# Two octets of a graph layer summed from SBUF instead of gathered: a change to a relational graph kernel

## The chip, the cores and the metric

The kernel runs on one core of one Trainium2 chip. The metric is device time in microseconds (us) from launch to end, the median of several executions. A profiled execution gives each engine's instructions with start and duration. The engines: TensorE (PE; its weight loads are PEld), VectorE (DVE), ScalarE (ACT), GpSimd (POOL) and SyncE (SP). "L766" is line 766 of the kernel's file.

## The reference

Two layers of a relational graph convolution with eight relations, 12500 nodes of 128 features and 200000 edges sorted by destination, then a residual and a layer norm:

```python
def _rgcn_conv(x, src, dst, et, basis, comp, root, bias):
    W = jnp.einsum('rb,bio->rio', comp, basis)
    xw = jnp.einsum('ni,rio->nro', x, W)
    msgs = xw[src, et]
    seg = dst * N_REL + et
    summed = segment_sum(msgs, seg, N_NODES * N_REL)
    cnt = segment_sum(ones, seg, N_NODES * N_REL)
    mean = summed / maximum(cnt, 1.0)[:, None]
    agg = mean.reshape(N_NODES, N_REL, HIDDEN).sum(axis=1)
    return agg + x @ root + bias
h = x
for l in range(2):
    h = relu(_rgcn_conv(h, ...)) + h
out = layernorm(x + h)
```

So each node takes, over its incoming edges, the source's row times the matrix of the edge's relation, divided by how many of its edges have that relation.

## The kernel before

The 200000 edges are cut into 1563 tiles of 128 edges, one edge per partition, and eight tiles make an octet (`Q = G = 8`, `NQ = 196` octets). The nodes are cut into 98 blocks of 128 (`NT`).

**Gathers.** For each tile GpSimd issues one indirect DMA that fetches 128 rows of 512 bytes, one per edge, into a slot of `rows` (L766, in `gather`, L738). A ring of seven buffers of one octet each holds them; in the main loop the gathers of octet q+5 are issued at octet q (`gathers`, L786), and an instruction of GpSimd waits until the buffer that it fills has been used. A few tiles are "lone": their rows are fetched one by one by SP and ACT (`lone_rows`, L679; 56 tiles of layer 1, 64 of layer 2). The last six octets are gathered under a tighter rule (`LATE`, `CLOSE`).

**Layer 1** gathers rows of x. For each tile VectorE makes a one-hot `dm` (L1188) from the numbers 0 to 127 (`cols`, which stand in PSUM), the edge's place `kr` (16 destinations x 8 relations) and its weight `w` (one over the count). TensorE multiplies rows and one-hot (`means`, L1288), which gives the means per destination and relation, turned; the relations' matrices follow (`product`, L1320), then a second one-hot `pl` puts the 128 results of an octet where their destinations belong (`place`, L1351). The result h is kept turned, features by nodes, in `hT`, a part of `arena` in SBUF. From h a table `y_d` in HBM is made with one row for each node and relation, h times the relation's matrix (`table`, L1408).

**Layer 2** gathers rows of `y_d` (index `idy`), so that a row is already a message. The loop at L1813 runs over the octets q: gathers of octet q+5, lone rows, `add_rows(q)` (L1447), `onehot(1, q + 2)` (L1844), then one step of the layer norm from `todo`. `add_rows` is eight matmuls on TensorE, row buffer times one-hot of 256 columns (`near`, L1463), summed in a PSUM accumulator `acc[k]`; a block of 128 nodes takes two octets, and opens with the node's own row times `root` (L1466). Three accumulators are used in turn (`acc_b`, L1443). When a block is complete, `finish` (L1359) adds the carry and the bias on VectorE and, one octet later, the ReLU and the residual (L1395). For every eight blocks `norm` (L1534) appends steps of the layer norm; one of them (L1571) is on ACT, and VectorE's L1575 waits for it.

**Order.** `Plan` (L300) writes out one order of instructions per engine, by hand: each engine takes its own in turn, and waits on semaphores for what others write or read. The one-hots have two buffers in layer 2, so `onehot(1, q + 2)` waits until the sums of octet q are done. From its column 128 x HA on, `arena` holds the edges' raw numbers in layer 1 (`early`, L524); `hT` takes 98 x 128 columns.

Of the kernel before, what the change touches and what calls it, by code (L numbers as in the profile page):

```python
# [299 lines left out]
class Plan:  # L300
# [90 lines left out]
    last = None  # L391
# [37 lines left out]
def ordered_path(  # L429
# [26 lines left out]
    P = 128  # L456
# [41 lines left out]
    def keep(shape, dtype, name):  # L498
        return const.tile(shape, dtype, name=name)
# [50 lines left out]
    def h_cells(j):  # L550

        return [("h", j)] + [c for a, b, cells in over.values() if a < (j + 1) * P and b > j * P for c in cells]

    comp_sb = keep([P, L * R * NB], F32, "comp_sb")
    first = keep([P, B], F32, "first")
# [50 lines left out]
    def vec(emit, reads=(), writes=()):  # L606
        plan.add("DVE", emit, reads, writes)
# [4 lines left out]
    def pe(emit, reads=(), writes=()):  # L612
        plan.add("PE", emit, reads, writes)
# [124 lines left out]
    def gather(l, q):  # L738
        if q >= NQ:
            return  # L740
# [419 lines left out]
    def rows_of(j):  # L1160
        return min(P, N - j * P)
# [11 lines left out]
    def onehot(l, q, g=None):  # L1173

        if q >= NQ and (g is None or g < 0):
            return
# [231 lines left out]
    def table(j):  # L1408
# [5 lines left out]
        def half(k):  # L1414
# [8 lines left out]
            def second_step(copy=copy):  # L1423
# [69 lines left out]
    def first_sums():  # L1493
# [4 lines left out]
        k = NT - 1  # L1498
        a, ac = acc[k] = acc_b[k % 3]
        m = rows_of(k)  # L1500
# [312 lines left out]
    for q in range(NQ):  # L1813
# [11 lines left out]
        if opens:  # L1825
            acc[k] = acc_b[k % 3]
        if q == NQ - 1:
# [105 lines left out]
```

## Time and profile before

| | |
|---|---|
| median of 3 executions | 3782.29 us (3776.45 to 3784.11) |
| the profiled execution's own time | 3776.47 us |
| its span, first to last instruction | 3774.6 us |
| granted TensorE clock, mean | 0.821 |
| POOL | busy 2840.8 us, 75% |
| TensorE matmuls | busy 2394.9 us, 63% |
| VectorE | busy 1692.9 us, 45% |
| ScalarE | busy 354.4 us, 9% |
| mean HBM traffic | 75 GB/s over the span |

Layer 2's gathers begin near 1890 us. A group's row reads: line, engine, operation, written tile `<-` read tiles, shapes, count `|` busy us, mean ns of one `|` idle time of the engine before them, and what ended it. In a timeline a row is start us, duration us, engine, line and operation. "Issue" is time in which an engine waited for nothing that the profile shows.

### The profile page before, as it was taken

To read this page: it belongs to the slowest core of one execution; us is meant where nothing else is said; L and a number is where in the kernel's file an instruction comes from. 1 tells how busy PE (TensorE), PEld (TensorE's weight loads), DVE (VectorE), ACT (ScalarE), POOL (GpSimd) and SP (SyncE) were. 2 spreads that over 40 slices of the span, in tenths; PEclk is the share of its full clock that TensorE was granted. 3 is DMA by queue.
4 is the path that set the end of the run, shared out by engine and by line. 5 is a ranking of instruction groups with operands and counts; after the bars stand their busy time and mean duration, and the time that the engine had idled before them with its cause. 6 is when DMAs were issued, how large, how long until landed. Compare 5 with 4: busy or idle time off the path is not lost.

```text
span 3774.6 us, 63987 instructions
## 1 busy us (share of the span) xinstructions
PE 2394.9 (63%) x11367; PEld 1919.0 (51%) x11367; DVE 1692.9 (45%) x4754; ACT 354.4 (9%) x795; POOL 2840.8 (75%) x3015
## 2 busy tenths in 40 slices
PE   5777657777767767776755654655555556565556
PEld 3566645555555556665544443444444445444344
DVE  5656424544434333343343443543544444444445
ACT  1111212211111111111100000000000000000000
POOL 7777777777777777777777777777777777777776
PEclk7999879999888888789887777877877777777777
DMA  4222233433323233323332222223223232232222
GB/s 125 56 62 62 56 89 102 126 106 106 100 79 89 84 89 89 84 83 96 93 86 55 56 61 62 61 62 67 61 62 67 56 67 62 61 68 61 62 61 69
DMA packets 157204, 286.78 MB, mean 76 GB/s; under 512 B 67548, under 2 KB 90846, under 8 KB 156790
## 3 DMA queue, kind: packets, MB, share of 16 engines
q0 software_dynamic: 96224, 197.26, 22.6%
q10 hardware_dynamic: 31051, 55.68, 4.5%
q1 hardware_dynamic: 29515, 29.70, 3.0%
q14 instruction: 322, 2.64, 0.2%
q8 instruction: 92, 1.51, 0.2%
HBM read 223.72 MB, written 58.65 MB: 75 GB/s over the span
## 4 chain that ended last, share of the span: by engine, by line
POOL 41%; issue 17%; DMA 14%; PE 9%; ACTq 8%; SPq 4%; ACT 3%; DVE 2%; POOLq 0%; DVEq 0%
POOL rows L766 41%; DMA rows<-y_d,idy 12%; ACTq L702 6%; SPq L702 4%; ACTq L697 2%; PE s L1288 2%; ACT sT L623 2%; PE y L1320 1%; PE pt L1418 1%; ACT y_row L623 1%; SPq L697 1%; PE s L1463 1%; DVE dm L1188 1%; PE ct L959 1%; PE ct L960 1%
## 5 line engine op out<-in xcount | busy, mean ns | idle before, releaser
L766 POOL DMA_INDIRECT rows<-in_x_dram,idx x1507 | 1423.9, 945 | 462.2 <-issue 455.8
L766 POOL DMA_INDIRECT rows<-y_d,idy x1499 | 1414.8, 944 | 457.6 <-issue 443.3
L1188 DVE TENSOR_SCALAR dm<-cols,near,w 128x256 f32<-128x256 f16 x1563 | 723.5, 534 | 749.2 <-PE s L1463 424.4
L1463 PE MATMUL s<-dm,rows 128*128 128x256 f32 x1984 | 627.9, 478 | 444.7 <-DMA rows<-y_d,idy 328.2
L1463 PEld LDWEIGHTS s<-dm,rows 128*128 128x128 f32 x1984 | 472.5, 247 | 569.9 <-issue 305.8
L1188 DVE TENSOR_SCALAR dm<-cols,kr,w 128x128 f32<-128x128 f16 x1563 | 525.3, 401 | 206.8 <-PE s L1288 177.3
L1288 PEld LDWEIGHTS s<-dm,rows 128*128 128x128 f32 x3014 | 435.9, 225 | 273.6 <-DMA rows<-in_x_dram,idx 222.7
L1288 PE MATMUL s<-dm,rows 128*128 128x128 f32 x3014 | 458.7, 312 | 171.9 <-DMA rows<-in_x_dram,idx 168.3
L1463 PE MATMUL ct<-dm,rows 128*128 128x256 f32 x1008 | 357.4, 521 | 305.0 <-DMA rows<-y_d,idy 190.1
L1463 PEld LDWEIGHTS ct<-dm,rows 128*128 128x128 f32 x1008 | 265.7, 274 | 379.2 <-issue 202.8
L1320 PE MATMUL y<-w_sb,sT 128*128 128x128 f32 x1968 | 264.9, 292 | 52.4 <-ACT sT L623 52.4
L1320 PEld LDWEIGHTS y<-w_sb,sT 128*128 128x128 f32 x1968 | 251.3, 207 | 61.4 <-ACT sT L623 60.3
L1418 PE MATMUL pt<-w_sb,arena 128*128 128x512 f32 (+1 forms) x386 | 227.1, 673 | 64.7 <-DVE y_row L626 43.9
L1351 PE MATMUL po<-pl,ys 128*128 128x256 f32 x392 | 140.1, 442 | 156.0 <-ACT sT L623 150.9
L623 ACT ACTIVATE sT<-s 128x512 f32<-128x512 f32 x391 | 213.4, 606 | 83.3 <-PE s L1288 83.0
L626 DVE COPY y_row<-pt 128x512 f32<-128x512 f32 x56 | 38.7, 691 | 365.5 <-PE pt L1418 365.5
L623 ACT ACTIVATE y_row<-pt 128x512 f32<-128x512 f32 (+1 forms) x139 | 83.0, 597 | 1043.3 <-PE s L1288 560.3
L1320 PE MATMUL ct<-w_sb,sT 128*128 128x128 f32 (+1 forms) x1168 | 162.3, 299 | 0.7 <-ACT sT L623 0.7
L1351 PEld LDWEIGHTS po<-pl,ys 128*128 128x128 f32 x392 | 65.3, 202 | 184.3 <-ACT sT L623 174.1
L1320 PEld LDWEIGHTS ct<-w_sb,sT 128*128 128x128 f32 (+1 forms) x1168 | 157.5, 216 | 1.3 <-ACT sT L623 1.1
L1571 ACT ACTIVATE st<-st,eps 128x8 f32<-128x8 f32 x12 | 3.7, 309 | 1560.3 <-DMA sT<-y_d 1507.0
L1372 DVE TENSOR_TENSOR po<-po,carry 128x128 f32<-128x128 f32 x98 | 29.0, 296 | 251.5 <-PE s L1288 230.4
(214 smaller groups left out, 1290.7 us busy)
## 6 DMA issues: line engine op xcount, KB each, us to landing
sT<-y_d SPq DMA_DIRECT2D x4096, 0.5 KB
sT<-y_d ACTq DMA_DIRECT2D x4096, 0.5 KB
y_d<-y_row ACTq DMA_DIRECT2D x96, 512.0 KB
mixer<-in_x_dram ACTq DMA_DIRECT2D x2304, 0.5 KB
rows<-in_x_dram,idx POOLq DMA_INDIRECT x1507
rows<-y_d,idy POOLq DMA_INDIRECT x1499
jmp<-in_x_dram SPq DMA_DIRECT2D x1408, 0.5 KB
comp_sb<-in_x_dram SPq DMA_DIRECT2D x1408, 0.5 KB
```

Of the source, the lines that this page charges most:

```text
L623: act(lambda: nc.scalar.activation(out_t, in_t, AF.Copy), reads, writes)
L626: vec(lambda: nc.vector.tensor_copy(out_t, in_t), reads, writes)
L697: _, at = nc.values_load_multi_w_load_instructions(offs[r:r + 1, l * P + j * ch:l * P + (j + 1) * ch], engines=[mybir.EngineType.SP if e = ...
L702: return [eng.dma_start(o[j * ch + i:j * ch + i + 1, :].bitcast(byte), table_b[bass.ds(v, 4 * D)].rearrange("(p d) -> p d", p=1)) for i, v ...
L766: ins.append(nc.gpsimd.indirect_dma_start(out=t[:, i - q * Q, :], out_offset=None, in_=table_t, in_offset=bass.IndirectOffsetOnAxis(ap=ids ...
L959: nc.tensor.matmul(ct[:, :nb, :], id_h, eq[:, s - s0, :nb, main], start=(s == 1), stop=False)
L1188: emits.append(lambda i=i: nc.vector.tensor_scalar(t[:, i - q * Q, :wide], cols[:, :wide], ids[:, i:i + 1], w[:, i:i + 1], op0=ALU.is_equa ...
L1288: last = nc.tensor.matmul(s_b[i // 4][0][:, i % 4, :], lones[i][0] if i in lones else t[:, i, :], d[:, i, :], start=True, stop=True)
L1320: last = nc.tensor.matmul(y[:m], t[:, r, :nt, :].rearrange("p t k -> p (t k)"), w_sb[:, 0, r, :], start=(r == 0), stop=(r == R - 1))
L1351: ins = nc.tensor.matmul(a, o[:m], t[:m], start=opens, stop=last and not root_in)
L1418: pe(lambda: nc.tensor.matmul(hb[:n].rearrange("p r d -> p (r d)"), hT[:, j * P:j * P + n], w_sb[:, 1, k * H:(k + 1) * H, :].rearrange("p ...
L1463: ins = nc.tensor.matmul(a, lones[i][0] if i in lones else t[:, i, :], d[:, i, :], start=(opens and i == 0), stop=(last and i == n - 1 and ...
```

## The change

Octets 96 and 188 of layer 2 (`SUMMED`, 16 tiles, none of them lone) are neither gathered nor given one-hots by `onehot`. Instead their rows are summed up from h in SBUF over many earlier octets: octet 96 during octets 3 to 86, octet 188 during 94 to 178. A load on SP brings the octet's 1024 source numbers to all partitions; VectorE casts them to float32 (`edge`). For each block j of 128 nodes TensorE turns `hT`'s block (`turn`), VectorE copies it out and makes a one-hot of 128 x 1024, block's node against edge's source (`ready`), and TensorE multiplies the two in two matmuls of 512 columns that accumulate over all 98 blocks (`sums`). At the end these sums, rows of h by edge, turned, go through the steps of layer 1 for that octet in the steps `done + 1` to `done + 7`, and `place_sums` adds the octet's result where `add_rows` would have summed the gathered rows. Buffers for it lie in `arena` behind `hT`. A PSUM bank each is taken by the turned blocks and by the two halves of the sums; for that layer 2's accumulators go from three to two, and `y` grows to a whole bank.

```diff
+    SUMMED = {96: (3, 86), 188: (94, 178)}
...
+    edge = later_on(Q * P)
+    hot_b = [(later_on(Q * P), ("hot", i)) for i in range(4)]
+    hn_b = [(later_on(P), ("hn", i)) for i in range(4)]
...
-    y_b = [(psum.tile([P, D], F32, name="y"), ("py", 0))]
+    y_full = (psum.tile([P, 4, P], F32, name="y"), ("py", 0))
+    y_b = [(y_full[0][:, 0, :], y_full[1])]
...
     def gather(l, q):
-        if q >= NQ:
+        if q >= NQ or l == 1 and q in SUMMED:
             return
...
     def onehot(l, q, g=None):
 
-        if q >= NQ and (g is None or g < 0):
+        if q >= NQ and (g is None or g < 0) or l == 1 and q in SUMMED:
             return
...
-             (s_b[1][0].rearrange("p t d -> p (t d)")[:, :2 * P], s_b[1][1]),
-             (ct_b[0].rearrange("p t d -> p (t d)")[:, :2 * P], ct_b[1])]
+             (s_b[1][0].rearrange("p t d -> p (t d)")[:, :2 * P], s_b[1][1])]
+
+    def summed(served, first, end):
+
+        n = end - first + 1
+        takes = {q: [] for q in range(first, end + 3)}
+        for j in range(NT):
+            takes[first + j * n // NT].append(j)
+        halves = (pt_b, y_full)
...
+        done = end + 2
...
+        def turn(q):
+            for j in takes.get(q, ()):
+                m = rows_of(j)
+                b, bc = ct_b
+                pe(lambda j=j, m=m, b=b: nc.tensor.transpose(b[:m, j % 4, :], hT[:, j * P:j * P + m], ident),
+                   [("h", j), "ident"], [bc])
+            plan.mark("PE")
+
+        def ready(q):
+            for j in takes.get(q - 1, ()):
+                m = rows_of(j)
+                (o, oc), (e, ec) = hn_b[j % 4], hot_b[j % 4]
+                vec(lambda j=j, m=m, o=o: nc.vector.tensor_copy(o[:m], ct_b[0][:m, j % 4, :]), [ct_b[1]], [oc])
+                vec(lambda j=j, e=e: nc.vector.tensor_scalar(e, edge, float(-j * P), part_f, op0=ALU.add,
+                                                             op1=ALU.is_equal), ["edge", "part_f"], [ec])
+            plan.mark("DVE")
+
+        def sums(q):
+            for j in takes.get(q - 2, ()):
+                m = rows_of(j)
+                (o, oc), (e, ec) = hn_b[j % 4], hot_b[j % 4]
+                for h, (b, bc) in enumerate(halves):
+                    pe(lambda j=j, m=m, o=o, e=e, h=h, b=b: nc.tensor.matmul(
+                        b.rearrange("p t c -> p (t c)"), o[:m], e[:m, 4 * h * P:4 * h * P + 4 * P],
+                        start=j == 0, stop=j == NT - 1), [oc, ec], [bc])
+
+        def before(q):
+            if q == first - 3:
+                load(g_t.bitcast(I32), bass.AP(tensor=src.tensor, offset=src.offset + served * Q * P,
+                                               ap=[[0, P], [1, Q * P]]), [], [g_c] + fresh)
+            if q == first + 1:
+                vec(lambda: nc.vector.tensor_copy(edge, g_t.bitcast(I32)), [g_c], ["edge"] + fresh)
+            ready(q)
+            if q == done + 1:
+                each_half(lambda h, b, bc: vec(lambda: nc.vector.tensor_copy(g3[:, 4 * h:4 * h + 4, :], b), [bc],
+                                               [g_c]))
+                vec(in_turn([lambda i=i, t=t: nc.vector.tensor_scalar(
+                    d3[:, i, :], cols[:, :P], kr[:, t:t + 1], w[:, t:t + 1], op0=ALU.is_equal, op1=ALU.mult)
+                    for i, t in enumerate(tiles)]), ["cols", ("kr", b0), ("wt", b0)], [d_c])
...
+        def after(q):
+            sums(q)
+            turn(q)
+            if q == done + 2:
+                each_half(lambda h, b, bc: pe(in_turn([lambda i=i: nc.tensor.transpose(
+                    b[:, i, :], g3[:, 4 * h + i, :], ident) for i in range(4)]), [g_c, "ident"], [bc]))
+            if q == done + 4:
+                each_half(lambda h, b, bc: pe(in_turn([lambda i=i: nc.tensor.matmul(
+                    b[:, i, :], r3[:, 4 * h + i, :], d3[:, 4 * h + i, :], start=True, stop=True)
+                    for i in range(4)]), [r_c, d_c], [bc]))
+            if q == done + 6:
+                pe(in_turn([lambda r=r: nc.tensor.matmul(
+                    y_full[0][:, 0, :], s4[:, r].rearrange("p t k -> p (t k)"), w_sb[:, 1, r, :],
+                    start=r == 0, stop=r == R - 1) for r in range(R)]),
+                   [s_c] + [("w", 1, r) for r in range(R)], [y_full[1]])
+            plan.mark("PE")
...
+    def place_sums(q, k, opens, last):
+        t, c = pl.pop(q)
+        o, oc = ys.pop(q)
+        a, ac = acc[k]
...
+            ins = nc.tensor.matmul(a, o, t, start=opens, stop=last and not root_in)
...
     def add_rows(q, k, opens, last, between_last=None):
+        if q in SUMMED:
+            place_sums(q, k, opens, last)
+            return
...
         if opens:
-            acc[k] = acc_b[k % 3]
+            acc[k] = acc_b[k % 2]
...
+        summing(q, 0)
         add_rows(q, k, opens, last)
         onehot(1, q + 2)
+        summing(q, 1)
```

`summing(q, 0)` calls `before(q)` and `summing(q, 1)` calls `after(q)` of the octet being summed.

More of the change, by code (lines that the diff above doesn't have):

```diff
@@ L552, in h_cells, with later_on @@
         return [("h", j)] + [c for a, b, cells in over.values() if a < (j + 1) * P and b > j * P for c in cells]
+    room = [NT * P]
+    room_c = [c for a, b, cells in over.values() if b > NT * P for c in cells]
+    def later_on(n):
+        room[0] += n
+        assert room[0] <= at
+        return arena[:, room[0] - n:room[0]]
+    edge = later_on(Q * P)
+    hot_b = [(later_on(Q * P), ("hot", i)) for i in range(4)]
+    hn_b = [(later_on(P), ("hn", i)) for i in range(4)]
     comp_sb = keep([P, L * R * NB], F32, "comp_sb")
@@ new lines, in ordered_path, with summing, emit @@
+    sums_of = [(s - 1, *summed(s, *SUMMED[s])) for s in sorted(SUMMED)]
+    def summing(q, part):
+        for end, *f in sums_of:
+            if SUMMED[end + 1][0] - 3 <= q <= end:
+                f[part](q)
+    def place_sums(q, k, opens, last):
+        t, c = pl.pop(q)
+        o, oc = ys.pop(q)
+        a, ac = acc[k]
+        root_in = opens and k >= 0
+        reads = [c, oc] + ([("h", k), ("w", 1, R)] if root_in else [])
+        def emit():
+            ins = nc.tensor.matmul(a, o, t, start=opens, stop=last and not root_in)
+            if root_in:
+                ins = nc.tensor.matmul(a[:, :rows_of(k)], w_sb[:, 1, R, :], hT[:, k * P:k * P + rows_of(k)],
+                                       start=False, stop=last)
+            return ins
+        pe(emit, reads, [ac])
+        plan.mark("PE")
@@ L1498, in first_sums @@
         k = NT - 1
-        a, ac = acc[k] = acc_b[k % 3]
+        a, ac = acc[k] = acc_b[k % 2]
         m = rows_of(k)
```

27 lines of the change are left out of this document (added).

## The prediction

> **What bounds the kernel now.** I read the page's busy shares and costliest groups first, then the stretches of layer 2, then the list of waits of GpSimd's engine.
>
> ```profile
> span 3774.6 us, 63987 instructions
> PE 2394.9 (63%) x11367; PEld 1919.0 (51%) x11367; DVE 1692.9 (45%) x4754; ACT 354.4 (9%) x795; POOL 2840.8 (75%) x3015
> L766 POOL DMA_INDIRECT rows<-in_x_dram,idx x1507 | 1423.9, 945 | 462.2 <-issue 455.8
> L766 POOL DMA_INDIRECT rows<-y_d,idy x1499 | 1414.8, 944 | 457.6 <-issue 443.3
> ```
>
> No engine is busy for more than 75%, yet POOL has no free time. Its 3006 gathers take 0.94 us each, and behind each lies a gap put down to "issue", so to nothing that another engine does. The second row gives (1414.8 + 457.6) / 1499 = 1.249 us from one gather to the next. The stretches (one of layer 1, then layer 2) and the waits say the same:
>
> ```profile
> core 0: us, PE busy (x) PEld busy (x) DVE busy (x) ACT busy (x) POOL busy (x), PEclk, DMA share, GB/s
> 400.00:800.00 400.00, 281.66 (x1633) 224.42 (x1634) 166.57 (x505) 72.07 (x160) 302.21 (x321) 0.88 0.34 96
> ...
> 2000.00:3600.00 1600.00, 892.85 (x2911) 703.05 (x2909) 732.70 (x1856) 4.37 (x11) 1208.87 (x1282) 0.76 0.29 62
> engine line waited for: us in total, times, longest us
> POOL rows L766 <- issue: 401.5, 1315, 0.3
> POOL rows L766 <- DMA rows<-y_d,idy: 12.2, 40, 0.3
> POOL rows L766 <- PE s L1463: 1.5, 5, 0.3
> ```
>
> 1600 us of layer 2 hold 1282 gathers, 1.248 us apiece, and no wait of POOL is longer than 0.3 us, which is the ordinary gap under another name. So layer 2 is one unbroken row of gathers: a gather left out is worth 1.249 us, and anything that lengthens a gather is paid in full. TensorE (56% here) and VectorE (46%) have room.
>
> **What the change removes.** 16 gathers that nothing delayed: 16 x 1.249 = 20.0 us, the whole gain. The 16 one-hots and 16 matmul pairs that go with them lie on engines with room and count nothing.
>
> **What it adds on VectorE, and what that does to POOL.** For each of 98 blocks of h, twice over, VectorE copies a turned block out of PSUM, and compares 1024 float32 source numbers in SBUF with the block's 128 rows into another SBUF tile: 196 compares, and two casts of the same width that fill `edge`, 198 wide operations. None of the trace is as wide. Its operations from SBUF to SBUF, with one turned out of PSUM for comparison:
>
> ```profile
> L1046 DVE TENSOR_SCALAR arena<-arena 128x128 f32<-128x128 f32 x13 | 2.9, 222 | 0.2
> L921 DVE CAST arena<-arena 128x512 f32<-128x512 int32 x3 | 1.2, 416 | 0.0
> L1578 DVE TENSOR_SCALAR x_g<-x_g,st 128x128 f32<-128x128 f32 x96 | 25.9, 357 | 0.4
> L626 DVE COPY y_row<-pt 128x512 f32<-128x512 f32 x56 | 38.7, 691 | 365.5 <-PE pt L1418 365.5
> ```
>
> From 128 to 512 columns it is (416 - 222) / 384 = 0.51 ns an element, half of what the copy out of PSUM needs (691 against 416 at the same width). That makes 222 + 896 x 0.51 = 0.68 us for 1024. The new compare has one operand that is a column (`part_f`); L1578 has two and takes 0.13 us more than L1046, so I add half, 0.06: 0.74 us. Bounds: 0.68 without it, 0.80 with both.
>
> The busy time is small (1.2 compares per octet). But these fast operations do something to POOL. Here are six places of the timeline (the profile merges neighbours of a kind); POOL's undisturbed row is 0.94 or 0.95:
>
> ```profile
> 288.60 0.61 DVE L938 TENSOR_SCALAR arena<-arena 128x896 int32<-128x896 int32 x1
> 288.77 1.26 POOL L766 DMA_INDIRECT rows<-in_x_dram,idx  x1 [0.30 <-issue]
> ...
> 698.91 0.22 DVE L1048 TENSOR_SCALAR arena<-arena 128x128 f32<-128x128 f32 x1
> 698.96 0.99 POOL L766 DMA_INDIRECT rows<-in_x_dram,idx  x1 [0.30 <-issue]
> ...
> 147.39 1.10 POOL L766 DMA_INDIRECT rows<-in_x_dram,idx  x1 [0.30 <-issue]
> 147.96 0.41 DVE L921 CAST arena<-arena 128x512 f32<-128x512 int32 x1
> ...
> 155.04 0.95 POOL L766 DMA_INDIRECT rows<-in_x_dram,idx  x1 [0.31 <-issue]
> 155.16 0.62 DVE L938 TENSOR_SCALAR arena<-arena 128x896 int32<-128x896 int32 x1
> ...
> 637.76 0.95 POOL L766 DMA_INDIRECT rows<-in_x_dram,idx  x1 [0.30 <-issue]
> 638.39 0.36 DVE L1048 TENSOR_SCALAR arena<-arena 128x128 f32<-128x128 f32 x1
> ...
> 2511.26 2.14 DVE L1578 TENSOR_SCALAR x_g<-x_g,st 128x128 f32<-128x128 f32 x8
> 2511.88 1.05 POOL L766 DMA_INDIRECT rows<-y_d,idy  x1 [0.30 <-issue]
> ```
>
> At 288.77 a gather starts while a fast operation runs, and is 0.32 us too long. The operation ends at 289.21; 289.21 - 0.32 is 0.12 us into the gather. At 698.96 the operation ends at 699.13, the gather loses 0.05: again 0.12. So about 0.12 us after its start a gather needs something that the operation holds, and waits for its end. At 147.39 the operation starts 0.57 into the gather and ends 0.98 into it, and the gather loses 0.16: a second need, at 0.98 - 0.16 = 0.82 at the latest. At 155.04 the operation runs from 0.12 to 0.74 of the gather, between the two, and nothing is lost; it started no later than the first need and did not stop it, so it holds nothing in its first part. At 638.39 it is the other way round: an operation that starts at 0.63 takes 0.36 and not 0.22, to 0.99, and the gather loses nothing. There POOL holds, from about 0.65 to 0.90 (0.14 late on a flow that would have begun near 0.78). The last pair shows it in layer 2: 1.05 for 0.94.
>
> So a 0.74 us compare holds for its last 0.56 us, say (0.51 ns x 1024 = 0.52 of flow, and its end). Its hold may begin anywhere in a gather's 1.249 us: VectorE's work hangs on landings and matmuls of varying length, and the rows above show it at every phase. In the three parts of a period:
> - beginning at A from 0.12 to 0.65, it ends at A + 0.56 and costs what lies beyond 0.82: 0 to 0.39 us, over the last 0.39 of that stretch, area 0.076;
> - from 0.65 to 0.90 it waits, then ends at 1.46, and the next gather wanted it at 1.37: 0.09 over 0.25, area 0.022;
> - from 0.90 to 1.37 it runs across the next gather's first need: 0.09 to 0.56, mean 0.325 over 0.47, area 0.153.
>
> The sum, 0.251, over 1.249 is 0.20 us per operation, and 198 x 0.20 = 39.8 us. Bounds: with the first need alone, that one row (147.39) being all that shows a loss at the second, 0.175 / 1.249 x 198 = 28 us; with 0.80 us long operations, a hold of 0.62, the same areas are 0.101, 0.038 and 0.181, so 51 us.
>
> The Trainium skill, SBUF — State Buffer, section Who interferes with whom, has a rule for this: a VectorE operation in a two-port mode and a GpSimd instruction take one shared port pair in turn, each for its whole instruction. The trace agrees that they exclude each other, but not on the whole instruction: the 0.62 us operation at 155.16 lies inside a gather and neither is longer for it. What the literal rule would make of the time is the second rival below.
>
> **TensorE.** Each block adds a turn and two matmuls of 512 columns.
>
> ```profile
> L1255 PE MATMUL pt<-ident,x_g 128*128 128x128 f32 x97 | 18.2, 317 | 14.8 <-DVE wide L626 12.8 <-ACT wide L623 1.2 <-DVE idx L898 0.8
> L1418 PE MATMUL pt<-w_sb,arena 128*128 128x512 f32 x384 | 226.0, 673 | 64.7 <-DVE y_row L626 43.9 <-DMA w_sb<-w_d 19.4 <-ACT y_row L623 1.4
> PE ct L1463 <- DVE dm L1188: 67.7, 10, 22.1
> 2514.52 16.10 DMA rows<-y_d,idy
> ```
>
> A float32 matmul is two instructions, so the turn is 2 x 18.2 / 97 = 0.38 us, a wide matmul 2 x 226.0 / 384 = 1.18, and a block 2.7 us. 98 blocks over 84 octets make 3.2 us per octet. An octet lasts 8 x 1499 / 1563 x 1.249 = 9.6 us, of which 56% or 5.3 are taken: 8.5 of 9.6. It fits. What covers it is the ring of seven row buffers: the gathers of octet n need the sums of octet n-7, whose rows land 16.1 us after they are issued (last row) and are then added in some 4 us, so POOL has 7 x 9.6 - 9.6 - 16 - 4 = 37 us of lead, against the longest stall of TensorE, 22 us.
>
> The accumulators go from three to two. A block's sums may now open only when VectorE has taken the block before last (the operation after `finish`), which stands one octet earlier in VectorE's queue than `onehot` two octets ahead. Behind it wait that octet's sums, and behind those POOL's buffers. In the stalls it makes TensorE stop an octet (4 us) earlier: 37 - 22 - 4 = 11 us are left. I take nothing; without the cover the price is the fourth rival's.
>
> `ready` stands in VectorE's queue before the one-hots two octets ahead and waits for the turn behind the previous sums; those one-hots wait for the next sums anyway, which lie later. The load of 512 KB on SP comes four octets, 38 us, before it is read. The closing steps of an octet (8 turns, 16 narrow and 2 x 8 instructions, copies from PSUM) take odd and even octets in turn, with no fast operation in them. The last octets, which set the tail, are unchanged.
>
> **The sum.** -20.0 + 39.8 = +19.8 us. The profiled execution took 3776.5 us (span 3774.6 and 1.9 around it): 3796.3. The median shown, 3782.3, lies 5.8 above that execution; I forecast 3799, in between. Slower, by about 0.5%.
>
> **Rivals.**
> 1. *No holding (faster).* The compare might run at the rate of operations that touch PSUM: then it holds nothing and POOL keeps its 1.249. The time is 3776.5 - 20.0 = 3756.5. For it: no operation with this pair of operands (a constant, then a column) is in the trace. Against: L1578, float32 with columns, does hold. It decides at a mean loss of 20.0 / 198 = 0.10 us per wide operation; above that the change loses.
> 2. *A gather keeps the place for its whole 0.94 us.* A compare that comes in those 76% waits for the gather's end, starts 0.30 us ahead of the next and keeps that one from 1.249 + 0.12 to 0.94 + 0.74: 0.31 us. One that comes in the gap costs 0.31 to 0.61, mean 0.46. Mean 0.35, times 198 is 68.7 us: 3825. Against it is the row at 155.16; for it that a stalled 638.39 ended just past its gather.
> These are the Trainium skill's words in that section, taken literally.
> 3. *Phase.* The compares fall into step with the gathers and mostly pass between the two needs, or mostly do not. Near nothing or 0.56 us each: 3757 to 3887; as both move with every octet's landing I expect the mean.
> 4. *TensorE becomes the bound after VectorE's stalls.* At 8.5 of 9.6 us an octet it gains 1.1 us an octet, 17 in the 16 octets between stalls of 22. What it can't make up, 5 us, would hold up POOL ten times: 50 us more, 3846. Against: TensorE was granted 0.76 of its clock here at 56%, but 0.88 in the quoted stretch of layer 1, where it was busy for 70%; a TensorE that catches up should be faster than 8.5.
>
> **How the numbers follow.** The forecast's own mechanism, with its bounds of 28 to 51 us and either base, 3784 to 3813: 0.66. Rival 1 with the good half of 3: 0.12. Rival 2: 0.10. Rival 4 and the bad half of 3: 0.08. The rest, 0.04, is a loss about equal to the gain. The range 3778 to 3826 takes in the first and the second of these with the last, and leaves the others, 0.20, outside. About 0.2%, 7.6 us, is what a measurement can tell from no change: faster 0.11, nearly all of the 0.12; the same 0.10, which is the 0.04, 0.05 from the lowest end of the forecast's mechanism, and 0.01 of the 0.12; slower 0.79, the rest.
>
> **What would show it.** POOL's gathers of layer 2 number 1483, and their mean rises from 944 to about 970 ns, with some reaching 1.5 us, from octet 3 to 178 and not outside; the gap of 0.30 stays. The compare's row says near 740 ns; at 1.3 us rival 1 holds. Stalled compares end about 0.99 into a gather. Waits of POOL for `rows` released by TensorE stay at 0.3 us; if some are of microseconds, rival 4 holds. The forecast is wrong if the gathers keep 944 ns.

## The result and the profile after

| | before | after |
|---|---|---|
| median | 3783.2 us (3776.45 to 3785.91, 4 executions) | 3828.26 us (3825.54 to 3831.74, 4 executions) |
| ratio of the times | | 1.0122 [1.0105, 1.014] |
| profiled execution, its own time | 3776.47 us | 3830.12 us |
| its span | 3774.6 us | 3828.3 us |

The kernel became 45.1 us slower, 1.2%; 3799 was forecast. The page of the kernel after, busy engines and the two groups of gathers:

```profile
span 3828.3 us, 66299 instructions
PE 2676.2 (70%) x12399; PEld 2044.1 (53%) x12399; DVE 1867.7 (49%) x5164; ACT 354.6 (9%) x795; POOL 2878.3 (75%) x2999
L780 POOL DMA_INDIRECT rows<-y_d,idy x1483 | 1449.3, 977 | 474.5 <-issue 439.3
L780 POOL DMA_INDIRECT rows<-in_x_dram,idx x1507 | 1427.0, 947 | 462.4 <-issue 455.6
```

Layer 2 has the 16 gathers fewer. Its gathers last 1449.3 / 1483 = 977.3 ns; those of layer 1, which the change does not touch, 1427.0 / 1507 = 946.9 in the same execution. The 30.4 ns between them, 1483 times, are 45.0 us. Then the stretches and the list of POOL's waits:

```profile
core 0: us, PE busy (x) PEld busy (x) DVE busy (x) ACT busy (x) POOL busy (x), PEclk, DMA share, GB/s
400.00:800.00 400.00, 281.62 (x1634) 223.48 (x1634) 168.23 (x509) 72.23 (x161) 302.54 (x320) 0.89 0.32 96
2000.00:3600.00 1600.00, 1147.77 (x3840) 813.06 (x3841) 889.52 (x2221) 4.39 (x11) 1203.95 (x1227) 0.86 0.27 60
```

```profile
engine line waited for: us in total, times, longest us
POOL rows L780 <- issue: 894.9, 2930, 0.3
POOL rows L780 <- PE s L1598: 26.1, 15, 21.8
```

Layer 1's stretch is as before. Layer 2's holds 1227 gathers where it held 1282, and a wait of 21.8 us that was not there. Beyond the ordinary gap of 0.3 us the waits of that row come to 26.1 - 15 x 0.3 = 21.6 us. So the budget of the change is -20.0 (the gathers left out) + 45.0 (longer gathers) + 21.6 (a wait) = +46.6, against 45.1 measured.

**Where the wait comes from.** Timelines of the kernel after around it: SP, then VectorE, then POOL.

```profile
1908.21 0.96 SPq L634 DMA_DIRECT2D x_g<-in_x_dram  x2
1914.25 99.74 SPq L716 DMA_DIRECT2D sT<-y_d  x256
2014.05 0.37 SPq L634 DMA_DIRECT2D arena<-in_src_dram  x1
```

```profile
2024.33 0.69 DVE L1510 CAST arena<-arena 128x1024 f32<-128x1024 int32 x1 [76.75 <-DMA arena<-in_src_dram]
...
2025.14 0.74 DVE L1492 TENSOR_SCALAR arena<-arena,part_f 128x1024 f32<-128x1024 f32 x1
...
2026.66 3.71 DVE L1202 TENSOR_SCALAR dm<-cols,near,w 128x256 f32<-128x256 f16 x8
```

```profile
2033.19 0.94 POOL L780 DMA_INDIRECT rows<-y_d,idy  x1 [21.80 <-PE s L1598]
```

The load of octet 96's source numbers is issued at 2014.05, because SP first issues 256 lone rows, 0.39 us each. VectorE waits 76.75 us for it, up to the cast that reads it, and the one-hots `dm` of the next octet stand behind the cast. POOL went on with the ring for the first 64 us of this wait and then stood for 21.80, so the ring covered some 55 of the 76.75 us.

**How a gather gets longer.** Four places of the same timeline, each a compare (L1492) and the gathers beside it:

```profile
2237.48 0.94 POOL L780 DMA_INDIRECT rows<-y_d,idy  x1 [0.30 <-issue]
2237.50 0.76 DVE L1492 TENSOR_SCALAR arena<-arena,part_f 128x1024 f32<-128x1024 f32 x1
...
2115.19 0.76 DVE L1492 TENSOR_SCALAR arena<-arena,part_f 128x1024 f32<-128x1024 f32 x1
2115.24 1.53 POOL L780 DMA_INDIRECT rows<-y_d,idy  x1 [0.30 <-issue]
...
3574.34 1.43 POOL L780 DMA_INDIRECT rows<-y_d,idy  x1 [0.30 <-issue]
...
3574.87 0.78 DVE L1492 TENSOR_SCALAR arena<-arena,part_f 128x1024 f32<-128x1024 f32 x1
...
3287.91 0.94 POOL L780 DMA_INDIRECT rows<-y_d,idy  x1 [0.30 <-issue]
...
3288.41 0.96 DVE L1492 TENSOR_SCALAR arena<-arena,part_f 128x1024 f32<-128x1024 f32 x1
3289.15 1.02 POOL L780 DMA_INDIRECT rows<-y_d,idy  x1 [0.30 <-issue]
```

At 2237.50 the compare lies inside a gather, ends 0.78 into it, and costs nothing. At 2115.19 it ends 0.71 into the gather that starts 0.05 after it: that one is 0.59 too long, so it needed the place at 0.12. At 3574.87 it ends 1.31 into its gather, which is 0.49 too long: needed at 0.82. At 3288.41 the gather comes first: the compare takes 0.96 instead of 0.76, ends 1.46 into the gather, and the next gather loses 0.08. So it is with all 196 compares of the trace: where the gather beside one is longer, it is longer by the compare's end less 0.82 us (its own gather) or less 0.13 (the next), to 0.015 us; where two compares meet one gather, the later sets it. Of the 35 that began 0.50 to 0.70 into a gather, 27 were held as at 3288.41, and 8 came in first. Of those that began just ahead of a gather, nine less than 0.048 us ahead cost nothing, and so did one at 0.084; the others from 0.048 on paid in full, as at 2115.19. So a compare holds nothing in about its first 0.05 + 0.12 = 0.17 us, near the 0.74 - 0.56 = 0.18 of the prediction.

### The profile page after: what moved, and what is told of

Read it like the earlier page. It is cut to its first block, busy times and chain, and to the rows that moved or that the text cites. A ratio compares the mean times of both kernels' runs of the same rounds, so it can differ in the third digit from the quotient of the medians.

```text
span 3828.3 us, 66299 instructions
## 1 busy us (share of the span) xinstructions
PE 2676.2 (70%) x12399; PEld 2044.1 (53%) x12399; DVE 1867.7 (49%) x5164; ACT 354.6 (9%) x795; POOL 2878.3 (75%) x2999
## 4 chain that ended last, share of the span: by engine, by line
POOL 44%; issue 18%; DMA 12%; PE 10%; ACTq 7%; SPq 3%; ACT 3%; DVE 2%; POOLq 0%; DVEq 0%
POOL rows L780 44%; DMA rows<-y_d,idy 10%; ACTq L716 5%; SPq L716 3%; PE s L1302 2%; ACTq L711 2%; PE s L1598 2%; ACT sT L637 2%; PE y L1334 1%; DVE dm L1202 1%; PE pt L1432 1%; PE ct L973 1%; PE ct L974 1%; ACT y_row L637 1%; SPq L711 1%
## 5 line engine op out<-in xcount | busy, mean ns | idle before, releaser
L780 POOL DMA_INDIRECT rows<-y_d,idy x1483 | 1449.3, 977 | 474.5 <-issue 439.3
L780 POOL DMA_INDIRECT rows<-in_x_dram,idx x1507 | 1427.0, 947 | 462.4 <-issue 455.6
L1598 PE MATMUL s<-dm,rows 128*128 128x256 f32 x2960 | 910.3, 467 | 495.4 <-DMA rows<-y_d,idy 470.9
L1598 PEld LDWEIGHTS s<-dm,rows 128*128 128x128 f32 x2960 | 683.5, 240 | 689.4 <-DMA rows<-y_d,idy 423.2
L1302 PEld LDWEIGHTS s<-dm,rows 128*128 128x128 f32 x3014 | 431.9, 224 | 297.9 <-DMA rows<-in_x_dram,idx 252.2
L1501 PE MATMUL y<-arena 128*128 128x512 f32 x392 | 200.2, 592 | 0.0
L1501 PE MATMUL pt<-arena 128*128 128x512 f32 x392 | 200.2, 592 | 0.0
```

The source lines that it names most:

```text
L780: ins.append(nc.gpsimd.indirect_dma_start(out=t[:, i - q * Q, :], out_offset=None, in_=table_t, in_offset=bass.IndirectOffsetOnAxis(ap=ids ...
L1302: last = nc.tensor.matmul(s_b[i // 4][0][:, i % 4, :], lones[i][0] if i in lones else t[:, i, :], d[:, i, :], start=True, stop=True)
L1501: pe(lambda j=j, m=m, o=o, e=e, h=h, b=b: nc.tensor.matmul(b.rearrange("p t c -> p (t c)"), o[:m], e[:m, 4 * h * P:4 * h * P + 4 * P], sta ...
L1598: ins = nc.tensor.matmul(a, lones[i][0] if i in lones else t[:, i, :], d[:, i, :], start=(opens and i == 0), stop=(last and i == n - 1 and ...
```

## The experiments

Every kernel is compared with the kernel before on the same chip. In three of the five sets of runs SP and ACT needed 0.6 us and more for a lone row instead of 0.38 to 0.45; lone rows then set the time, the kernel before takes 6016 to 6021 us, and those runs are told apart below. The view at the outset was that the three terms of the budget are independent and add up; the rivals were that the wait comes from TensorE's added work or from the missing accumulator, and that the saved gathers are given back elsewhere.

### The load ahead of the lone rows

Octet 96's load moves ahead of the first lone rows; octet 188's stays where it was.

```diff
-            if q == first - 3:
+            if q == first - 3 and served != min(SUMMED) or q == "load":
...
+            if q == "load":
+                return
...
+    sums_of[0][1]("load")
     for n in range(2):
```

> Early load alone, again, since in the first four runs SP took 0.6 us to issue a lone row where it takes 0.38 us in the profile before, lone rows and not POOL set the time (6017 us for the kernel before), and only the gathers' own durations could be read. Where SP issues at 0.38 us: theory A 3828 - 22 = 3806 us, POOL's wait gone; rival C 3828 us.

Measured: 3805.75 us against 3783.94, ratio 1.0057 [1.004, 1.0074]. Groups and waits of this kernel:

```profile
L780 POOL DMA_INDIRECT rows<-y_d,idy x1483 | 1448.1, 976 | 453.0 <-issue 440.2
```

```profile
POOL rows L780 <- PE s L1600: 2.1, 7, 0.3
```

The wait is gone and nothing else moved: the gathers keep their 976 ns. The load behind the lone rows was the whole of the wait. TensorE carries its added work, on two accumulators, without a wait of POOL above 0.3 us: as causes of lost time in the changed kernel those two rivals fall.

### The compare without a hold

The compare takes the node numbers of the block as a column that stands in PSUM, and becomes an operation of two tensors.

```diff
+    node_p = bank[:, P:P + NT].bitcast(F32)
...
-                vec(lambda j=j, e=e: nc.vector.tensor_scalar(e, edge, float(-j * P), part_f, op0=ALU.add,
-                                                             op1=ALU.is_equal), ["edge", "part_f"], [ec])
+                vec(lambda j=j, e=e: nc.vector.tensor_tensor(e, edge, node_p[:, j:j + 1].to_broadcast([P, Q * P]),
+                                                             op=ALU.is_equal), ["edge", "node_p"], [ec])
...
+            if q == first - 2 and served == min(SUMMED):
+                vec(lambda: nc.vector.tensor_scalar(node_p, cols[:, :NT], float(P), part_f, op0=ALU.mult,
+                                                    op1=ALU.add), ["cols", "part_f", "keyp"], ["node_p", "keyp"])
```

With the early load as well:

> Early load and column in PSUM, again, for its time. Theory A: 3757 to 3763 us, gathers of layer 2 at 944 ns. Rival C: 3779. If TensorE's added work costs something beside, the time lies between.

Measured: 3779.96 us (3776.45 to 3781.48) against 3783.94 (3782.01 to 3785.57), ratio 0.9989 [0.9979, 0.9998].

```profile
L781 POOL DMA_INDIRECT rows<-y_d,idy x1483 | 1403.4, 946 | 471.1 <-issue 437.4
...
L1493 DVE TENSOR_TENSOR arena<-arena,cols 128x1024 f32<-128x1024 f32 x196 | 237.2, 1210 | 0.0
```

```profile
POOL rows L781 <- PE s L1604: 22.3, 14, 9.9
```

The compare is longer, 1.21 us for 0.76, and holds nothing: gathers of 946 ns, as in layer 1 (947). But the kernel gains 4.0 us and not 20, for POOL now waits 22.3 - 14 x 0.3 = 18.1 us for rows buffers, most of it in two places: 8.7 us follow octet 188's load, still behind lone rows, and 9.9 stand ahead of octet 190. The time is the 3779 that rival C named; whether its cause is at work the next kernel tells.

### The saved gathers alone

Of the 98 blocks only the first is summed for each octet (97 are left out), with the early load: what is left of the change is 16 gathers fewer.

```diff
-        for j in range(NT):
-            takes[first + j * n // NT].append(j)
+        takes[first].append(0)
...
-                        start=j == 0, stop=j == NT - 1), [oc, ec], [bc])
+                        start=True, stop=True), [oc, ec], [bc])
```

> One block of 98, 97 left out, again, for its time: 16 gathers fewer and nothing else. Theory A: 3783 - 20 = 3763 us, and within 8 us of the run with both changes.

Measured: 3781.24 us, ratio 0.9994 [0.9985, 1.0004].

```profile
L780 POOL DMA_INDIRECT rows<-y_d,idy x1483 | 1404.5, 947 | 468.8 <-issue 440.0
```

```profile
POOL rows L780 <- PE s L1602: 19.0, 11, 9.3
```

A miss, and the one that taught most: with 97 of 98 blocks gone the time is that of the kernel with all of them (3779.96). So the blocks' matmuls, copies and compares cost nothing that can be measured once they hold nothing, and 16 gathers fewer gain 2.7 us here, which the interval (5.7 gained to 1.5 lost) does not tell from none: 19.0 - 11 x 0.3 = 15.7 us come back as waits. They stand at the same two places, 6.9 us behind octet 188's late load and 9.3 ahead of octet 190, so TensorE's added work does not make them; the two accumulators are in this kernel too. Octet 188's load is late here too, so this kernel alone doesn't show what the gathers are worth without it; the kernels with both loads early, below, do.

### Halves of the compare

Each compare is cut in two of 512 columns; early load.

```diff
+                vec(in_turn([lambda j=j, e=e, i=i: nc.vector.tensor_scalar(
+                    e[:, i:i + Q * P // 2], edge[:, i:i + Q * P // 2], float(-j * P), part_f, op0=ALU.add,
+                    op1=ALU.is_equal) for i in range(0, Q * P, Q * P // 2)]), ["edge", "part_f"], [ec])
```

> Early load, and each fast compare cut into two of 512 columns, one behind the other: the same port, the same columns, a hold of some 0.32 us and not 0.58, twice as often. Theory A: what a hold costs grows with its square; worked out as in the prediction, 0.32 long holds cost about 0.06 us each, 392 of them 24 us and not 49, so 3806 - 25 = 3781 us; less would say that POOL slips in between the two. Rival (what counts is the columns that pass through the port): 3806 us.

Measured: 3794.52 us, ratio 1.0028 [1.0018, 1.0038].

```profile
L780 POOL DMA_INDIRECT rows<-y_d,idy x1483 | 1425.5, 961 | 460.5 <-issue 435.8
```

```profile
POOL rows L780 <- PE s L1601: 11.9, 14, 7.9
```

Layer 1's gathers took 1427.8 / 1507 = 947.4 ns here, so the excess is 13.8 ns, 20.4 us, or 0.052 us for each of 392 compares, where a whole one costs 0.22. Twice as many that cost a quarter: a hold of half the length both meets a need half as often and lasts half as long past it. The gathers' part, 22.9 us less than with whole compares, is near the 25 expected; the time fell by 11 only, as 7.7 us of waits came in, ahead of octet 190.

### Both operands in SBUF

As the column in PSUM, but with the column in SBUF, and with both loads early (the second octet is 180 here, as in the next experiment).

```diff
-    node_p = bank[:, P:P + NT].bitcast(F32)
+    node_p = later_on(NT)
```

> As the first of these, but the compare's column lies in SBUF too: an operation with two inputs in SBUF, at one element a cycle, with the same columns and nearly the same duration, 1.2 us. If only the fast mode holds up gathers: 3764 us, gathers at 947 ns. If two SBUF inputs hold too, for about 1.1 us, but only against a gather's first need (0.12 us after its start): by the prediction's way about 0.48 us each, 196 x 0.48 = 95 us, 3859 us. If against both needs: 0.73 us each, 144 us, 3908 us.

Measured: 3836.42 us against 3776.86, ratio 1.0161 [1.0145, 1.0177]. The page, and one place of the timeline:

```profile
L781 POOL DMA_INDIRECT rows<-y_d,idy x1483 | 1482.2, 999 | 452.6 <-issue 438.9
L781 POOL DMA_INDIRECT rows<-in_x_dram,idx x1507 | 1425.0, 946 | 462.4 <-issue 456.0
```

```profile
2449.37 0.94 POOL L781 DMA_INDIRECT rows<-y_d,idy  x1 [0.30 <-issue]
...
2449.86 1.21 DVE L1495 TENSOR_TENSOR arena<-arena 128x1024 f32<-128x1024 f32 x1
...
2450.61 1.28 POOL L781 DMA_INDIRECT rows<-y_d,idy  x1 [0.30 <-issue]
```

The same operation with a second input from SBUF costs 53.9 ns a gather, 80 us in all or 0.41 each, of the 0.48 expected for the first need alone. At 2449.86 it runs across the 0.82 us of its own gather, which stays at 0.94, and delays only the next: it ends 0.46 into that one, which is 0.34 too long. Over the whole trace 180 of the 196 compares lengthen the next gather, each by its end less 0.12 to 0.13 us, and none its own gather by what lies beyond 0.82. It conflicts with the first need and not with the second, so the two needs are of different kinds.

The Trainium skill, SBUF — State Buffer, section Who interferes with whom, says that a VectorE operation outside the two-port modes contends with GpSimd only where it has two inputs in SBUF, and then only with what GpSimd reads there. The runs agree: 946 ns with one input in SBUF, 999 with two. By that rule the need at 0.12 to 0.13 us would be a read and the one at 0.82 a write; no run shows which they are.

### Where the saved gathers go

Both loads early, with the column in PSUM. The second load goes, four octets into the first octet's sums, to a buffer of `table` that is free by then:

```diff
+        raw, raw_c = (g_t, [g_c]) if fresh else (
+            yr_r.tiles[1].rearrange("p r d -> p (r d)"), [("y_row", 1, 0), ("y_row", 1, 1)])
...
+        for i in range(1, len(sums_of)):
+            s = sums_of[i][0] + 1
+            if q == SUMMED[sums_of[i - 1][0] + 1][0] + 4:
+                sums_of[i][1](("load", s))
         summing(q, 0)
```

Octet 188 as before:

> As the last, but octet 188 stays. Theory A: the wait seven octets behind octet 96 goes, the one ahead of octet 190 stays at some 9 us, 3764 + 9 = 3773 us. Rival D: 3780 us.

and octet 180 in its place, to move it away from the end:

```diff
-    SUMMED = {96: (3, 86), 188: (94, 178)}
+    SUMMED = {96: (3, 86), 180: (94, 170)}
```

> Column in PSUM, both loads issued far ahead (octet 180's numbers into a y_row buffer, 83 octets before their cast), and octet 180 in place of 188. With both changes before, the time was 3780 us and not 3763: POOL waited 8.7 us seven octets behind octet 96, after a cast that waited 47 us for the second load behind SP's lone rows, and 9.9 us ahead of octet 190, whose gathers wait for the sums of octet 187 by the rule for the last octets. Theory A (these two waits gave the gain back): both gone, 3784 - 20 = 3764 us, no wait of POOL over 0.3 us. Rival D (lone rows, which SP and ACT issue nearly without pause, set the pace of layer 2, and POOL waits elsewhere instead): 3780 us with waits at other octets.

Measured against 3776.86 us: 3778.38, ratio 1.0003 [0.9994, 1.0012], and 3781.77, ratio 1.0013 [1.0004, 1.0022]. POOL's waits, first of octet 188, then of octet 180:

```profile
POOL rows L781 <- PE s L1605: 26.3, 15, 22.0
```

```profile
POOL rows L781 <- PE s L1605: 29.8, 11, 26.7
```

The two waits of the kernel with one early load became one of 22.0 and 26.7 us near the end: with the loads out of the way the saved time is still given back, all at once. Around that wait in the kernel with octet 180, VectorE's waits and the timeline:

```profile
DVE st L1717 <- ACT st L1713: 360.3, 12, 39.9
```

```profile
3599.90 107.15 ACTq L717 DMA_DIRECT2D sT<-y_d  x246
3707.10 0.31 ACT L1713 ACTIVATE st<-st,eps 128x8 f32<-128x8 f32 x1 [156.66 <-DMA sT<-y_d]
...
3707.44 0.20 DVE L1717 RECIPROCAL st<-st 128x8 f32<-128x8 f32 x1 [31.25 <-ACT st L1713]
...
3711.47 1.22 PE L1605 MATMUL s<-dm,rows 128*128 128x256 f32 x2 [28.40 <-DVE dm L1203]
...
3717.63 0.94 POOL L781 DMA_INDIRECT rows<-y_d,idy  x1 [26.74 <-PE s L1605]
```

and the same step in the kernel before:

```profile
3599.97 105.10 ACTq L702 DMA_DIRECT2D sT<-y_d  x234
3705.12 0.31 ACT L1571 ACTIVATE st<-st,eps 128x8 f32<-128x8 f32 x1 [158.54 <-DMA sT<-y_d]
...
3705.46 0.21 DVE L1575 RECIPROCAL st<-st 128x8 f32<-128x8 f32 x1 [6.97 <-ACT st L1571]
```

The chain reads upwards from the gather: it waits for sums, these for one-hots, these stand behind the layer norm's reciprocal on VectorE, that waits for ACT's step, and ACT's step stands behind its lone rows, which it issues without a pause, 105.10 / 234 = 0.45 us apiece. ACT ends that row 2 us later than in the kernel before, though POOL has 16 gathers fewer. In the kernel before VectorE came to the reciprocal at 3698.5 and waited 7 us, which the ring hid; in this one it comes at 3676.2, 22 us earlier, and waits 31.

That this wait reaches POOL just here points to a second reason. In all six kernels with a late wait it stands ahead of the same gather, the first of octet 190, and that octet is the first of the last six, whose gathers are issued two octets ahead and not five (`CLOSE`, `LATE`). VectorE's earlier waits for ACT's step in this kernel, up to 39.9 us, cost POOL nothing: its other waits for sums are of 0.3 us. The missing accumulator takes part in the kernel with octet 188: there TensorE's last wait ahead of octet 190, 10.53 us, is for `wide` (L1410, the ReLU and the residual), which frees one of the two accumulators and stands behind the same reciprocal. No kernel leaves out gathers with three accumulators or without the last octets' rule, so their shares aren't shown.

One octet more, three in all:

```diff
-    SUMMED = {96: (3, 86), 188: (94, 178)}
+    SUMMED = {62: (3, 52), 122: (60, 112), 180: (120, 170)}
```

> As the first of these with three octets, 62, 122 and 180, in 50 octets each, two blocks an octet. If POOL is still all that sets the time: 3784 - 30 = 3754 us. If TensorE and VectorE become the bound where they carry two blocks an octet beside the sums (by the prediction's rows 5.3 + 2 x 2.7 = 10.7 us of an octet's 9.6): waits of POOL for rows, no gain over two octets or a loss.

Measured: 3783.27 us, ratio 1.0015 [1.0006, 1.0024].

```profile
POOL rows L781 <- PE s L1605: 41.3, 13, 36.1
```

Ten microseconds of gathers more taken out, and the one wait is ten longer. What stays is the time at which ACT comes to its step behind the lone rows. With one block, then with three octets:

```profile
3706.82 0.31 ACT L1710 ACTIVATE st<-st,eps 128x8 f32<-128x8 f32 x1 [156.02 <-DMA sT<-y_d]
```

```profile
3708.08 0.31 ACT L1713 ACTIVATE st<-st,eps 128x8 f32<-128x8 f32 x1 [154.89 <-DMA sT<-y_d]
```

It comes at 3705.1 us in the kernel before and at 3706.4 to 3709.3 in the five kernels without held gathers, whether 16 gathers are left out or 24, and the spans of all six end 69 to 74 us behind it. The terms of every kernel of these two sets, each worked out as above (gathers left out at 1.249 us; mean of layer 2 less mean of layer 1, times their count; waits less 0.3 each):

| kernel | left out | longer gathers | waits | sum | measured |
|---|---|---|---|---|---|
| early load | -20.0 | +43.3 | 0 | +23.3 | +21.8 |
| halves | -20.0 | +20.4 | +7.7 | +8.1 | +10.6 |
| column in PSUM, early load | -20.0 | -1.6 | +18.1 | -3.5 | -4.0 |
| one block | -20.0 | -0.6 | +15.7 | -4.9 | -2.7 |
| both loads, octet 188 | -20.0 | -1.0 | +21.8 | +0.8 | +1.5 |
| both loads, octet 180 | -20.0 | -1.3 | +26.5 | +5.2 | +4.9 |
| column in SBUF | -20.0 | +79.9 | +0.1 | +60.0 | +59.6 |
| three octets | -30.0 | -1.5 | +37.4 | +5.9 | +6.4 |

Where the gathers are held by 43 us or more there is no wait; where they are not, the wait takes back what was saved. The terms do not add up freely.

### Fewer lone rows

If ACT's and SP's lone rows are a second clock, two lone tiles fewer should free it. One tile each is given back to the gathers from SP's and ACT's lists (of 64):

```diff
-        [("SP", 62, 1552, 47, 32, 15, [(floats(sT_f[0], j), [("sT", 0, 0), ("sT", 0, 1)], []) for j in range(4)]),
-         ("ACT", 63, 1552, 48, 32, 15, [(floats(sT_f[1], j), [("sT", 1, 0), ("sT", 1, 1)], []) for j in range(4)])]]
+        [("SP", 62, 1519, 47, 32, 15, [(floats(sT_f[0], j), [("sT", 0, 0), ("sT", 0, 1)], []) for j in range(4)]),
+         ("ACT", 63, 1551, 48, 32, 15, [(floats(sT_f[1], j), [("sT", 1, 0), ("sT", 1, 1)], []) for j in range(4)])]]
```

In octet 180's kernel (two summed octets), ACT's list alone, three summed octets, and the kernel before:

> Two octets summed (96 and 180), column in PSUM, both loads early, and the last lone tile of layer 2 of SP and of ACT given back to POOL. The run without this moved POOL's waits to one of 26.7 us ahead of octet 190, behind TensorE, VectorE and a step of the layer norm on ACT that stands behind ACT's last lone row at 3707 us; in the kernel before ACT issues its last lone row at 3705 us as well. Theory E (ACT's 4096 lone rows, 0.438 us apiece without a pause, are a second clock of layer 2, as long as POOL's gathers): ACT ends 56 us earlier, the wait goes, 3777 - 20 + 2 x 1.25 = 3760 us. Rival (the wait is TensorE's or the last octets' rule): 3782 us or more.

> As the last, but only ACT's last lone tile is given back; SP keeps its own, whose last row it issues at 3700 us for octet 189. Theory E with ACT alone: 3758 us. If SP's rows are a third clock: the wait moves to the sums of octet 189, some 10 us, 3768 us.

> Three octets summed (62, 122, 180) with both lone tiles given back. Theory E: 3777 - 30 + 2.5 = 3750 us. If TensorE and VectorE, with two blocks an octet, become the bound: waits of POOL through the layer, 3760 us or more.

> The kernel before, with the two lone tiles given back and nothing else. Theory E: POOL and ACT were equally long, so POOL's two more gathers are paid and ACT's shorter list buys nothing: 3777 + 2.5 = 3779 us. If ACT's list had been the bound of the kernel before: faster than 3777 us.

and two of them again:

> Again, as in the last four runs SP and ACT took 0.6 us and more to issue a lone row and these rows alone set the time (6016 us for the kernel before). Where a lone row takes 0.44 us: theory E, the last octets' wait goes: 20.0 - 2.5 = 17.5 us under the kernel before, 3760 us at a 3777 of it. Rival: 3780 us.

> Again, three octets. Theory E: 27.5 us under the kernel before, 3750 us at a 3777 of it. If TensorE and VectorE become the bound at two blocks an octet: waits of POOL through the layer, no better than two octets.

All six fell into sets with slow lone rows. One row of SP's timeline, of the kernel before with fewer lone rows, then of the kernel before as quoted at the outset:

```profile
2030.16 79.38 SPq L702 DMA_DIRECT2D sel<-in_x_dram  x128
```

```profile
318.52 48.60 SPq L702 DMA_DIRECT2D sel<-in_x_dram  x128
```

79.38 / 128 = 0.62 us against 0.38, so none of these times can be read against its expectation. As ratios to 6015.99 and 6020.51 us: two octets 0.988 [0.9859, 0.99] and again 0.9857 [0.9833, 0.9882]; ACT's alone 0.9919 [0.9898, 0.994]; three octets 0.9729 [0.9705, 0.9753] and 0.9709 [0.9686, 0.9732]; the kernel before with two lone tiles fewer 0.9926 [0.9906, 0.9946]. So with slow rows they are the clock: giving two tiles back to POOL makes even the kernel before faster, although POOL then issues two gathers more. For rows of 0.44 us this isn't shown: no run with such rows has a shorter list on ACT, or the layer norm's step on another engine. There the second clock is argued from the timelines above.

### The first set

The first four were also made in a set with slow lone rows (before: 6017.43 us):

> The changed kernel with the load of octet 96's source numbers put on SP ahead of the first lone rows of layer 2; nothing else differs. Theory A (two costs: the load stood behind 256 lone-row DMAs, VectorE's cast waited 76.8 us for it and POOL 21.8 us behind that; and the wide compares hold up gathers for 49 us): the wait goes, the gathers stay at a mean of 977 ns, 3828 - 22 = 3806 us. Rival C (POOL's wait comes from TensorE's added work and the two accumulators, with or without the load): a wait of some 20 us stays, 3828 us.

> The changed kernel with each compare written as a tensor_tensor of edge (SBUF) with a column of node numbers in PSUM, at one element a cycle, some 1.2 us and not 0.76; the load stays late. Theory A: an operation with one SBUF input outside the fast mode holds nothing, the gathers of layer 2 return to 944 ns though VectorE works longer, and 49 us go: 3828 - 49 = 3779 us, with POOL's one wait of some 22 us left. Rival B (gathers are slowed by the added work on VectorE and TensorE as such): they stay at 977 ns or rise, 3828 us or more.

> Early load and the column in PSUM together. Theory A: only the 16 gathers are left as an effect, 3828 - 22 - 49 = 3757 us by the changed kernel, 3783 - 20 = 3763 by the kernel before; faster than both. Rival B: 3806. Rival C: 3779.

> Early load, and only block 0 of the 98 is turned, compared and summed for each of the two octets; 97 blocks of each are left out, the gathers stay away, the closing steps stay. It measures what 16 gathers are worth alone. Theory A: 16 x 1.249 = 20.0 us, 3763 us, gathers at 944 ns, and within 0.2% of the run with both changes, as 97 more blocks cost nothing there. Rival (the gain is not what 16 gathers take, or TensorE's added work costs something): another time, or a gap to that run of over 8 us.

Ratios: early load 0.9902 [0.9868, 0.9936], column in PSUM 0.9916 [0.989, 0.9942], both 0.9933 [0.9905, 0.9961], one block 0.9911 [0.9884, 0.9938]. The times tell nothing apart, as POOL waited for sums for some 1000 us in each. The means of layer 2's gathers do: 960 ns with the early load alone, 943, 944 and 944 in the others. What makes all four 1% faster there was not followed up.

## Why the prediction was off

**Right: what the compares do to the gathers.** Wide fast operations lengthen POOL's gathers by two needs, forecast at 0.12 and 0.82 us into a gather and found at 0.13 and 0.82. The held compares end at 1.46, as the sum had it; the 0.99 in the list of signs was the end of a 128-column operation and did not fit. Forecast were 39.8 us, 0.20 for each of 198; measured 45.0, or 0.23, and 43.3 (0.22) with the early load: inside its bounds of 28 and 51. Halves, the column in PSUM and both operands in SBUF confirm the mechanism.

**Wrong: the load that was counted as nothing.** The step that failed is "The load of 512 KB on SP comes four octets, 38 us, before it is read." It is placed four octets ahead in the code, but on a queue that works in order, behind 256 lone rows. The trace of before had the price:

```profile
1911.34 148.74 SPq L702 DMA_DIRECT2D sT<-y_d  x378
```

0.39 us a row without a pause, so 100 us for 256, where 38 were allowed. Less the ring's cover this cost POOL 21.6 us; moving the load took 22.5 us off (3828.26 to 3805.75, in two sets whose kernels before differ by 0.7). With that and the 5 us of size the forecast's +19.8 becomes the +46.6 of the budget.

**Right in the sum, wrong as a rule: a gather left out is worth 1.249 us.** In the changed kernel the sum holds with it, as the held gathers keep POOL behind ACT: with the early load VectorE waits 81.5 us in all for ACT's step, against 244.9 in the kernel before. Without held gathers, 16 fewer gained 4.0 us at best and nothing with both loads early. The view that "POOL has no free time" was true, but ACT's lone rows keep the same pace, as the timelines have it, and the list of POOL's waits could not show it while VectorE's waits for ACT stayed inside the ring's lead: 12 waits of up to 34.9 us, against the 37 us worked out for the lead and the 55 that it covered in the kernel after.

```profile
DVE st L1575 <- ACT st L1571: 244.9, 12, 34.9
```

**Right in the changed kernel: what was costed at nothing elsewhere.** The accumulators and TensorE's blocks showed no price there, in a stretch where TensorE was busy for 1147.77 of 1600 us, 72%, less than the 8.5 of 9.6 allowed for it. Its granted clock went from 0.76 to 0.86, and a block took 2.3 us and not 2.7: four wide instructions, 400.4 / 196 = 2.04, and the turn, 48.8 / 194 = 0.25, which is one instruction and not the two that the prediction counted.

**The rivals.** The first (no holding) would have gained 20.0; the column in PSUM, which holds nothing, gained 4.0. The second's 3825 lies nearest to the result, but for another reason: the compare at 2237.50 shares a gather's 0.94 us at no cost. The third (phase) did not come: the compares met the gathers at every phase. Its upper end leaves out the 20.0 us saved: 198 x 0.56 less 20.0 gives 3867 and not 3887. The fourth (TensorE) did not come: the sign named for it, a wait of POOL of microseconds, appeared, but it was the load's.

Where a lone row takes 0.38 to 0.45 us, no version here clearly beats the kernel before: the best, column in PSUM with one early load, has 0.9989 [0.9979, 0.9998].

## What to carry to other kernels

A load's lead is counted from the moment when its queue can issue it: add up what stands ahead of it there, at the row's own price. An unbroken row on one engine doesn't prove that it alone sets the pace; look for a second queue that also issues without a pause, and for waits on it that only a buffer hides, before pricing what a removal is worth. Where a wide VectorE operation holds what GpSimd needs, cut it (0.22 us for 1024 columns, 0.052 for 512: about the square of the length), or make it one with one operand in PSUM (no price for the gathers here).

## What was not expected of the hardware

- A wide compare with one input in SBUF and one in PSUM takes 1.21 us and leaves the gathers at 946 ns; with both in SBUF, at the same 1.21 us, they take 999; the shorter form of 0.76 us, 976.
- A gather holds off VectorE only for a part of its 0.94 us: the compare that began 0.50 into it was held and ended 1.46 into it, the one that began at 0.02 wasn't.
- The issue of a 512-byte row on SP took 0.38 us in some sets and 0.62 in others, enough to take the same kernel from 3777 to 6017 us, while a gather's 944 to 947 ns hardly changed.
- TensorE's granted clock in layer 2 was higher where it was busier: 0.74 at 55% (one block), 0.76 at 56% (before), 0.86 at 72% (after), 0.87 at 75% (three octets).
